# Attention scores from two-part float32r queries and keys, three products of 64 rows by 128 columns, with the image buffers placed behind attention

## The chip, the cores and the metric

The kernel runs on one core of a Trainium2 chip. A core has a matrix engine (TensorE, "PE" in the profile, with its weight loads listed apart as "PEld"), a vector engine ("DVE"), a scalar engine for activations and copies ("ACT"), a general engine ("POOL"), and a queue engine that mostly starts transfers ("SP"). Each engine works through its own list of instructions in order and waits on semaphores for the others. Data lie in SBUF (128 partitions), matrix products go to PSUM (128 partitions by 8 banks; one bank holds 512 float32 per partition), and DRAM is reached by DMA. The metric is the device time of one execution in microseconds. All runs named here agree within 0.3%.

## The reference

The input `x` is one image of 48 channels by 128 by 128 pixels in float32. Four layers are applied, each as `x = x + layer(groupnorm(x))`: an attention over pixels, four sweeps of a 5-tap convolution over rows and columns, a patch-wise convolution with normalisation, and a state-space scan. The change lies in the first layer, which is:

```python
qkv = jnp.einsum('bchw,oc->bohw', x, qkv_w)                  # 48 -> 144 channels
qkv = conv_general_dilated(qkv, dw_w, ..., 'SAME', ...)      # 3x3 depthwise
q, k, v = jnp.split(qkv, 3, axis=1)                          # 16384 tokens of 48 each
q = _l2norm(q)
k = _l2norm(k)
attn = jnp.einsum('bnc,bmc->bnm', q, k) * temperature
attn = jax.nn.softmax(attn, axis=-1)                         # 16384 x 16384
out = jnp.einsum('bnm,bmc->bnc', attn, v)
return jnp.einsum('bchw,oc->bohw', out, proj_w)
```

So every one of 16384 queries meets every one of 16384 keys: two products, each of 16384 by 16384 by 48, with an exponential between them.

## The kernel before

The program lays the four layers one after another: `attention`, `sweeps`, `patch_conv`, `scan`. Two large SBUF buffers, `xa` and `xb`, are handed from one to the next (a layer calls them `xq` and `other`).

**Inside `attention`, the convolution stage.** The image is loaded by eight DMAs into `xb`, the first half of the rows in partitions 0 to 47, the second in 64 to 111. The stage then works in eight bands of 16 rows; each band in two iterations of 1024 tokens (two chunks of `CH` = 512). `band(b)` normalises 18 rows on DVE (line 93), and copies them by DMA into shifted partitions. `conv` makes q, k and v of the 1024 tokens on PE in plain float32. `take` squares them on ACT, sums over channels on PE (the matrix `blk`), takes the root on ACT, and then DVE does, per chunk, `tensor_scalar_max` (L300), `reciprocal` (L302), and two products that write the scaled q into `xq` and k into the lower half of `xb` (L304, L307). One iteration later ACT copies q a second time, into partitions 64 to 127 of `xq` (`again`). The keys thus lie in two halves: tokens 0 to 8191 in partitions 0 to 63, the others in 64 to 127, and the queries in both.

**The attention loop, `attend`.** It runs over 32 chunks `c` of 512 queries, and inside over 64 key tiles `j`. A key tile is 128 keys of each half. `scores(c, j)` makes, in four float32 products of 49 rows by 64 columns (the four quarters of the array), a PSUM tile `s` of 128 partitions by 2 by 512; ACT makes `e = exp(absT * s)` of it; `sums(acc, j, e)` multiplies it by the values, again in four products of 64 by 64, which accumulate over `j` in the PSUM tile `acc`. PE's order is written out by `InOrder`: the scores of tile `j`, then the sums of tile `j - 2` (`BEHIND`). There are three `s` tiles (six banks), one `acc` (two banks), and five `e` buffers. At the end of a chunk ACT copies `acc` to `o`, and `divide` and `result` (DVE, with small DMAs on SP) make the chunk's output, which stays in `xq` for the sweeps and goes by DMA to `x1` in DRAM. A second loop, `attend_shifted`, stands in the other branch of `tc.If` and isn't executed with this temperature.

**After attention.** `sweeps` takes group statistics (line 71 and on), keeps PE at work meanwhile with `keep_running` (line 99), fills the borders of its buffer by POOL memsets (L678 to L683), and ACT writes the normalised image from `xq` into `xb`, 8 rows at a time. The weights `l1_w` were loaded at the program's start.

Of the kernel before, what the change touches and what calls it, by code (L numbers as in the profile page):

```python
# [20 lines left out]
F16 = mybir.dt.float16  # L21
AF = mybir.ActivationFunctionType
# [4 lines left out]
C = 48  # L27
H = W = 128
N = H * W
# [76 lines left out]
def packed_weights(nc, pool, name, w, dw, cols):  # L106

    w1 = pool.tile([128, 4, cols], F32, name="w1")
    nc.scalar.dma_start(w1.rearrange("c t o -> c (t o)"), w)
    wt = pool.tile([128, 4, cols], F32, name=name)  # L110
    nc.scalar.dma_start(wt.rearrange("c t o -> c (t o)"), dw)
    nc.vector.tensor_mul(wt, wt, w1)
    return wt
# [6 lines left out]
def attention(ctx, tc, xq, other, x1, const, ins):  # L120
# [4 lines left out]
    ident, blk, st = const["ident"], const["blk"], const["st"]  # L125
    NQ = N // CH
    HALF = N // 2

    kv = ctx.enter_context(tc.tile_pool(name="l0_kv", bufs=1))

    k = other[:, 0:HALF]

    v = other[:, HALF:N].rearrange("p (t c) -> p t c", c=64)
# [11 lines left out]

    rp = ctx.enter_context(tc.tile_pool(name="l0_r", bufs=2))
# [3 lines left out]
    with ExitStack() as a:  # L150
        act, pe = InOrder(tc, nc.scalar), InOrder(tc, nc.tensor)
        wp = a.enter_context(tc.tile_pool(name="l0_w", bufs=1))
        sp = a.enter_context(tc.tile_pool(name="l0_a", bufs=2))
        ps = a.enter_context(tc.tile_pool(name="l0_aps", bufs=4, space=PSUM))
# [4 lines left out]
        wt = packed_weights(nc, wp, "wt", ins["l0_w"], ins["l0_dw"], 192)  # L159

        values = wt[:, :, 128:192]
        turned = wp.tile([64, 4, 128], F32, name="turned")
# [9 lines left out]
        K2 = 64 + C  # L172
        for i in range(NQ // 2 - 4):
            idle = ps.tile([128, CH], F32, name="p")
            keep_running(pe, idle, ident[0:K2], other[0:K2, i * CH : (i + 1) * CH], 1)
        halves = wp.tile([K2, NQ // 2, 6], F32, name="halves")
        for i in range(NQ // 2):
            nc.vector.bn_stats(halves[:, i, :], other[0:K2, i * CH : (i + 1) * CH])
# [3 lines left out]
        R = 16  # L182
        NB = H // R
        S = W + 2
        bands = [wp.tile([128, R + 2, S], F32, name=f"band{i}") for i in range(2)]
        rests = [wp.tile([128, R // 8, 4, W], F32, name=f"rest{i}") for i in range(2)]
# [3 lines left out]
        def band(b):  # L190
# [8 lines left out]
            for p0, p1 in [(0, 10), (10, R + 2)] if b == 0 else [(0, R + 2)]:  # L199
                for half, x in enumerate((other[0:C], other[64 : 64 + C])):  # L200
                    lo = max(first + p0, half * H // 2)
                    hi = min(first + p1, (half + 1) * H // 2)
                    if lo < hi:
                        at = half * H // 2
                        normalise(
                            nc,
                            t[0:C, lo - first : hi - first, 1 : W + 1],
                            rows(x[:, (lo - at) * W : (hi - at) * W]),
                            stats,
                        )  # L210
# [59 lines left out]
        def take(t0, p, pv):  # L270
# [5 lines left out]
            vt = sp.tile([128, CH], F32, name="vt")  # L276
# [21 lines left out]
            def scale():  # L298
                for n in range(2):
# [3 lines left out]
                    q = slice(t0 + n * CH, t0 + (n + 1) * CH)  # L303
                    nc.vector.scalar_tensor_tensor(  # L304
                        xq[0:64, q], p[n][0:64], sgn[0:64], rn[0:64], ALU.mult, ALU.mult
                    )
                    nc.vector.tensor_mul(  # L307
                        k[kb : kb + 64, tk + n * CH : tk + (n + 1) * CH], p[n][64:128], rn[64:128]
                    )
                nc.gpsimd.memset(k[kb + 32 : kb + 33, tk : tk + 2 * CH], 1.0)  # L310

            def again(copy):
                for n in range(2):
                    q = slice(t0 + n * CH, t0 + (n + 1) * CH)
                    copy(xq[64:128, q], xq[0:64, q])

            if p is not late:
                scale()
            nc.vector.tensor_copy(v[:, tv, :].rearrange("t (n i) c -> t i n c", n=2), pt)
            nc.gpsimd.memset(v[:, tv, C:64], 1.0)  # L320
            return scale, again
# [3 lines left out]
        for b in range(NB):  # L325
            nxt = band(b + 1) if b + 1 < NB else None
            for y in range(0, R, 8):
# [4 lines left out]
                if last:  # L332
                    last[1](act.copy)
# [4 lines left out]

    small = nc.values_load(absT[0:1, 0:1].bitcast(mybir.dt.int32))
    bits = int(np.float32(32.0).view(np.int32))  # L340
    with tc.If(small <= bits) as near:
        attend(tc, xq, k, v, x1, absT, ident, st, ins, last)
    with near.Else():
        attend_shifted(tc, xq, k, v, x1, absT, ident, st, ins, last)
# [17 lines left out]
def attend(ctx, tc, xq, k, v, x1, absT, ident, st, ins, last):  # L362
# [6 lines left out]
    act, pe = InOrder(tc, nc.scalar), InOrder(tc, nc.tensor)  # L369
    NQ = N // CH  # L370
    KT = N // 2 // 128
    BEHIND = 2

    ep = ctx.enter_context(tc.tile_pool(name="l0_e", bufs=BEHIND + 3))
# [9 lines left out]
    def scores(c, j):  # L384
        s = ps_s.tile([128, 2, CH], F32, name="s")
        for part, half, _ in quarters:
            b = 64 * half
            pe.matmul(
                s[part, half, :],
                lhsT=k[b : b + GAP, j * 128 + part.start : j * 128 + part.stop],  # L390
                rhs=xq[b : b + GAP, c * CH : (c + 1) * CH],
                start=True,
                stop=True,
            )
# [15 lines left out]
    class Finish:  # L410
# [24 lines left out]
        def result(self):  # L435
            y = self.y[0:C]
            nc.vector.tensor_mul(y, y, self.rec)
            nc.vector.tensor_add(xq[0:C, self.cols], y, self.xres)
            nc.vector.bn_stats(st[:, self.c, :], xq[0:C, self.cols])
            if self.c < NQ - 1:  # L440
                nc.sync.dma_start(x1[:, self.cols], xq[0:C, self.cols])
# [1401 lines left out]
```

## Time and profile before

| what | us |
|---|---|
| median of three runs (7403.55 to 7419.28) | 7405.37 |
| profiled execution, its own time | 7415.31 |
| its span, first to last instruction | 7413.5 |
| start and statistics of the image | 0 to 35 |
| convolution stage | 35 to 247 |
| attention loop | 247 to 3768 |
| end of attention to the first sweep | 3768 to 3785.5 |
| sweeps and patch convolution | 3785.5 to 4700 |
| scan | 4700 to 7413.5 |

The stages were cut where the first and last products of each lie in the timeline. In the listing of instruction groups, a row gives the line, the engine and operation, the result and its inputs, the shapes, the count, then the busy time of the group in us, the mean of one in ns, and the idle time of that engine ahead of it with what ended it. Line 48 is the helper `InOrder`, through which most PE and ACT instructions are issued, so rows are told apart by their tiles. A float32 product stands in the records as two MATMULs, so the 8192 score products of the program are 16384 rows. The duration of one MATMUL contains its latency; what PE needs for one is read from the distance of starts in the timeline.

### The profile page before, as it was taken

The page shows a single profiled execution, that of the slowest core. Times are in us where ns is not written, and L with a number is a line of the kernel's source. Part 1 is how long each engine was busy: PE and PEld are TensorE (multiplying, and loading weights), DVE is VectorE, ACT ScalarE, POOL GpSimd, SP SyncE. Part 2 cuts the span into 40 slices and gives each one's busy share as a digit, 9 for nine tenths or more (in the row PEclk, how much of TensorE's full clock was granted, in tenths as well). Part 3 has the DMA queues.
Part 4 walks back from the last instruction along what each step waited for, and adds up shares of the span by engine and source line. Part 5 has one row for each costly group of instructions (what it writes and reads, how often), then busy time and mean ns, then how long its engine had stood idle before and what let it go on. Part 6 is the DMA issues. An engine that isn't in the chain of part 4 may idle for free.

```text
span 7413.5 us, 220408 instructions
## 1 busy us (share of the span) xinstructions
PE 6051.7 (82%) x101970; PEld 3057.1 (41%) x101970; DVE 3451.0 (47%) x3031; ACT 4389.3 (59%) x4744; POOL 2804.1 (38%) x603
## 2 busy tenths in 40 slices
PE   8999999999999999999999999455555545554555
PEld 3333333333333333333357855243444333343444
DVE  7300000000000000000034544699999999999998
ACT  2566666666666666666644023566666666666665
POOL 1000000000000000000010222599999999999998
PEclk9999999999999999999999999677667767766666
DMA  3000000000000000000000020465566566666775
GB/s 67 8 4 5 4 3 4 5 3 4 4 3 5 4 3 4 5 3 5 4 11 20 3 49 18 108 165 151 166 156 165 152 159 160 162 158 165 180 179 146
DMA packets 182436, 485.73 MB, mean 66 GB/s; under 512 B 35971, under 2 KB 67762, under 8 KB 179602
## 3 DMA queue, kind: packets, MB, share of 16 engines
q1 hardware_dynamic: 174679, 464.21, 24.6%
q8 instruction: 799, 13.09, 0.8%
q10 hardware_dynamic: 6827, 7.35, 0.4%
q14 instruction: 131, 1.07, 0.1%
HBM read 427.91 MB, written 22.02 MB: 61 GB/s over the span
## 4 chain that ended last, share of the span: by engine, by line
PE 61%; DVE 22%; issue 7%; POOL 5%; ACT 2%; DMA 2%; SPq 0%; ACTq 0%; DVEq 0%; POOLq 0%
PE acc L48 24%; PE s L48 24%; DVE h L1590 20%; PE p L48 7%; POOL h L1583 4%; PE y L48 3%; DMA du<-rep 1%; PE pv L48 1%; PE pp L48 1%; PE pc L48 1%; PE po L48 1%; DVE xb L48 1%; ACT dA L48 1%; ACT xb L48 1%; DVE y L48 0%
## 5 line engine op out<-in xcount | busy, mean ns | idle before, releaser
L48 ACT ACTIVATE e<-s,absT 128x1024 f32<-128x1024 f32 x2048 | 2279.5, 1115 | 1194.9 <-PE s L48 1194.0
L1583 POOL TENSOR_TENSOR h<-du,bt 128x3072 f32<-128x3072 f32 (+1 forms) x386 | 2559.9, 6676 | 94.2 <-ACT h L48 47.4
L48 PE MATMUL s<-xa,xb 49*64 49x512 f32 x16384 | 2118.1, 588 | 1.3 <-POOL xb L320 1.3
L48 PE MATMUL acc<-e,xb 64*64 64x512 f32 x16384 | 2118.1, 588 | 1.0 <-ACT e L48 1.0
L1590 DVE TENSOR_TENSOR_SCAN h<-dA,carry,h 128x1024 f32<-128x1024 f32 x864 | 1940.5, 2324 | 49.1 <-ACT dA L48 33.7
L48 ACT ACTIVATE dA<-dt,a 128x1024 f32<-128x1024 f32 x1152 | 1287.2, 1118 | 868.1 <-DVE h L1590 856.9
L48 PE MATMUL y<-h,cw 128*32 128x48 f32 x49152 | 905.9, 246 | 954.2 <-issue 513.8
L421 DVE TENSOR_TENSOR both<-o 128x512 f32<-128x512 f32 x31 | 21.5, 692 | 2963.2 <-ACT o L48 2859.5
L681 POOL MEMSET xb<- 32x2064 f32 x8 | 14.5, 1818 | 3500.4 <-PE acc L48 3491.3
L48 PEld LDWEIGHTS y<-h,cw 128*32 128x32 f32 x49152 | 815.1, 140 | 1081.6 <-issue 672.9
L48 PEld LDWEIGHTS s<-xa,xb 49*64 49x64 f32 x16384 | 616.0, 132 | 1146.1 <-issue 588.9
L48 PEld LDWEIGHTS acc<-e,xb 64*64 64x64 f32 x16384 | 615.7, 132 | 1146.8 <-issue 1123.3
L1590 DVE TENSOR_TENSOR_SCAN h<-dA,h 128x1024 f32<-128x1024 f32 x288 | 634.5, 2268 | 46.0 <-ACT dA L48 37.6
L48 PE MATMUL yz<-ev,sel 128*8 128x48 f32 x4096 | 192.1, 259 | 267.9 <-ACT ev L48 266.7
L48 PEld LDWEIGHTS yz<-ev,sel 128*8 128x8 f32 x4096 | 162.3, 106 | 326.1 <-ACT ev L48 296.4
L48 PE MATMUL p<-xb,l_w 112*48 112x78 f32 (+8 forms) x6096 | 227.5, 224 | 19.3 <-DVE xb L48 8.9
L48 PE MATMUL p<-xa,l_w 112*48 112x78 f32 (+8 forms) x6096 | 227.5, 224 | 14.4 <-DVE xa L48 5.5
L48 PEld LDWEIGHTS p<-xb,l_w 112*48 112x48 f32 x6096 | 194.5, 124 | 52.9 <-DVE xb L48 35.4
L48 PEld LDWEIGHTS p<-xa,l_w 112*48 112x48 f32 x6096 | 193.8, 123 | 48.1 <-DVE xa L48 33.7
L48 PE MATMUL pc<-wt,xa 128*128 128x288 f32 x768 | 198.0, 415 | 0.0
L783 POOL TENSOR_TENSOR xb<-xb,xa 48x2048 f32<-48x2048 f32 (+2 forms) x10 | 45.0, 4503 | 386.4 <-DVE xa L48 363.2
L48 DVE TENSOR_TENSOR xb<-p,xb 112x79 f32<-112x79 f32 (+7 forms) x508 | 114.6, 226 | 129.4 <-PE p L48 113.5
(204 smaller groups left out, 3106.3 us busy)
## 6 DMA issues: line engine op xcount, KB each, us to landing
du<-rep SPq DMA_DIRECT2D x768, 256.0 KB
dt<-rep SPq DMA_DIRECT2D x768, 256.0 KB
rep<-dd SPq DMA_DIRECT2D x24, 192.0 KB
yd<-ys ACTq DMA_DIRECT2D x256, 12.0 KB
rest<-xa SPq DMA_DIRECT2D x90, 38.0 KB
xb<-in_x_dram SPq DMA_DIRECT2D x8, 384.0 KB
xres<-in_x_dram SPq DMA_DIRECT2D x32, 96.0 KB
x<-xa SPq DMA_DIRECT2D x32, 96.0 KB
```

What stands on the lines that cost most here:

```text
L48: ins = method(*args, **kwargs).ins
L421: nc.vector.tensor_add(self.both, o[:, 0], o[:, 1])
L681: nc.gpsimd.memset(b[32:64, some, inside], 1.0)
L783: nc.gpsimd.tensor_add(xr, xr, u[0:C, x : x + xr.shape[2], E : E + H].rearrange("c w h -> c h w"),)
L1583: nc.gpsimd.tensor_mul(h[:, p, ks], du.unsqueeze(1).to_broadcast([128, ks.stop - ks.start, LC]), r["bt"][:, ks],)
L1590: nc.vector.tensor_tensor_scan(h[:, p, k, :], dA, h[:, p, k, :], carry[:, i, k : k + 1] if ci else 0.0, ALU.mult, ALU.add,)
```

## The change

Queries and keys are each split on the chip into a high part, rounded to `float32r`, and the rest, also `float32r`: `hq`, `lq`, `kh`, `kl`. A score is then made of three products in place of one: `kh` with the high query, `kl` with the high query, and both key parts with the low query. 64 rows are used in each: the channel order of q and k is turned (16 to 47, 0 to 15, and 0 to 15 once more), so that the third product and parts of the first two share rows; for the third, 32-row pieces of `kh` and `kl` are put below one another in the tiles `rest_k`. Each product now covers 64 rows by all 128 columns, and the two key halves take the upper and lower rows of the array.

The parts of the query go to a DRAM buffer `qm`, from which `moving(c)` loads a chunk by eight DMAs, one chunk ahead. Order on PE: the scores of `G` = 4 key tiles, then the sums of the four tiles before. There are seven `e` buffers. The sums are as they were. The image lies in four tiles of its own, `xa` and `xb` are laid out only after attention, the sweeps read the attention's result back from `x1` through two stage buffers, and `l1_w` is loaded after attention.

```diff
-def attention(ctx, tc, xq, other, x1, const, ins):
+def attention(ctx, tc, x1, mp, const, ins):
+    images = ctx.enter_context(tc.tile_pool(name="l0_x", bufs=1))
+    for i in range(HALF // PART):
+        t = images.tile([128, PART], F32, name=f"x{i}")
...
+    kh, kl = (kv.tile([128, HALF], F32R, name=n) for n in ("kh", "kl"))
+    def moving(c):
+        m = mp.tile([128, 2, CH], F32R, name="m")
+        high, low = qm[0:C, c * CH : (c + 1) * CH], qm[C:, c * CH : (c + 1) * CH]
+        for half in range(2):
+            at = 64 * half
+            for i, to, x in (
+                (0, 0, high),
+                (0, C, low[C:]),
+                (1, 0, low[0:32]),
+                (1, 32, low[0:32]),
+            ):
+                nc.sync.dma_start(m[at + to : at + to + x.shape[0], i].bitcast(F32), x)
+        return m
+    def join(cols):
...
+        for half in range(2):
+            at = 64 * half
+            for n, t in enumerate((kh, kl)):
+                nc.sync.dma_start(
+                    rest_k[i][at + 32 * n : at + 32 * n + 32, to].bitcast(F32),
+                    t[at : at + 32, cols].bitcast(F32),
+                )
...
+                for half in range(2):
+                    for i, x in enumerate(image):
+                        at = half * H // 2 + i * PART // W
+                        lo = max(first + p0, at)
+                        hi = min(first + p1, at + PART // W)
+                        if lo < hi:
+                            normalise(
...
-                nc.gpsimd.memset(k[kb + 32 : kb + 33, tk : tk + 2 * CH], 1.0)
-            def again(copy):
-                    copy(xq[64:128, q], xq[0:64, q])
+            def split(act, get):
+                for n in range(2):
+                    f = own[n]
+                    hq, lq = (get(name, n)[qb : qb + 64] for name in ("hq", "lq"))
+                    fq, fk = f[qb : qb + 64], f[kb : kb + 64]
+                    act.copy(hq.bitcast(F32R), fq)
+                    act.copy(kh[kb : kb + 64, at], fk)
+                    nc.gpsimd.tensor_sub(lq.bitcast(F32R), fq, hq)
+                    nc.gpsimd.tensor_sub(kl[kb : kb + 64, at], fk, kh[kb : kb + 64, at].bitcast(F32))
+                    nc.sync.dma_start(qm[0:C, to], hq[0:C])
+                    nc.sync.dma_start(qm[C : 64 + C, to], lq)
+                if kb:
+                    join(slice(tk, tk + 2 * CH))
+            def get(name, n):
+                pool = {"f": fp, "hq": once, "lq": sp}[name]
+                return pool.tile([128, CH], F32, name=name)
...
-    def scores(c, j):
+    def scores(m, j):
         s = ps_s.tile([128, 2, CH], F32, name="s")
-        for part, half, _ in quarters:
-            b = 64 * half
-            pe.matmul(
-                s[part, half, :],
-                lhsT=k[b : b + GAP, j * 128 + part.start : j * 128 + part.stop],
-                rhs=xq[b : b + GAP, c * CH : (c + 1) * CH],
+        for n in range(3):
+            k, at = key_tile(keys, n, j)
+            for half, part in enumerate(sides):
+                pe.matmul(
+                    s[:, half, :],
+                    lhsT=k[part, at],
+                    rhs=m[part, n // 2],
+                    start=(n == 0),
+                    stop=(n == 2),
...
-        for j in range(KT):
-            waiting.append((c, j, scores(c, j)))
-            while len(waiting) > BEHIND:
+        for g in range(KT // G):
+            es = [(j, scores(m, j)) for j in range(g * G, (g + 1) * G)]
+            if g == 0 and c + 1 < NQ:
+                ahead = moving(c + 1)
+            if c == 0 and g == 1:
+                split(act, get)
+            for i, e in behind:
+                if i == 0:
+                    acc = ps_a.tile([128, 2, CH], F32, name="acc")
+                sums(acc, i, e)
+            if c and g == 0:
+                finish = Finish(c - 1, acc)
...
+def key_tile(keys, n, j):
+    if n < 2:
+        return keys[n], slice(j * 128, (j + 1) * 128)
+    per = keys[2][0].shape[1] // 128
+    return keys[2][j // per], slice(j % per * 128, (j % per + 1) * 128)
...
-    keep_running(nc.tensor, idle, const["ident"], some, 6)
+    idle, some = idle[:, 0:128], const["blk"]
+    keep_running(nc.tensor, idle, const["ident"], some, 16)
...
+    for r in range(0, H, 8):
+        x = stage.tile([128, 2, CH], F32, name="m").rearrange("c a b -> c (a b)")[0:C]
+        nc.sync.dma_start(x, x1[:, r * W : (r + 8) * W])
...
-        attention(tc, xa, xb, x1, const, ins)
+    stage = ctx.enter_context(tc.tile_pool(name="stage", bufs=2))
+    attention(tc, x1, stage, const, ins)
     with ExitStack() as image:
         xp = image.enter_context(tc.tile_pool(name="image", bufs=1))
         const["l1_w"] = xp.tile([128, 3, 3, 64 + C], F32, name="l1_w")
+        nc.sync.dma_start(const["l1_w"], ins["l1_w"])
...
-    blk[:64, :64] = blk[64:, 64:] = 1.0
+    blk[:C, :64] = blk[64 : 64 + C, 64:] = 1.0
+    def turned(a):
+        return np.concatenate([a[:, 16:], a[:, :16], a[:, :16]], 1)
```

The branch that isn't executed, `attend_shifted`, is changed in the same sense. `patch_conv` and `scan` keep their work; the first rows of their hand-over, `const["x3"]`, lie in the two stage buffers in place of a buffer of their own.

## The prediction

> **What bounds the kernel now.** I read the busy time by stage first (columns: stretch in us; its length, then busy time and instruction count of PE, PEld, DVE, ACT, POOL; granted clock; DMA share; GB/s):
>
> ```profile
> core 0: us, PE busy (x) PEld busy (x) DVE busy (x) ACT busy (x) POOL busy (x), PEclk, DMA share, GB/s
> 247.00:3768.00 3521.00, 3520.10 (x32744) 1230.69 (x32744) 217.04 (x197) 2323.94 (x2113) 12.81 (x13) 1.00 0.02 4
> 35.00:247.00 212.00, 209.62 (x672) 78.18 (x672) 186.37 (x150) 66.11 (x114) 21.20 (x32) 0.97 0.24 42
> ```
>
> Attention is 3521 of 7413.5 us, and PE is busy in all of it at clock 1.00; ACT has a third of its time free and DMA is nearly idle. The groups of instructions say what PE does there and that it hardly ever waits:
>
> ```profile
> L48 ACT ACTIVATE e<-s,absT 128x1024 f32<-128x1024 f32 x2048 | 2279.5, 1115 | 1194.9 <-PE s L48 1194.0
> ...
> L48 PE MATMUL s<-xa,xb 49*64 49x512 f32 x16384 | 2118.1, 588 | 1.3 <-POOL xb L320 1.3
> L48 PE MATMUL acc<-e,xb 64*64 64x512 f32 x16384 | 2118.1, 588 | 1.0 <-ACT e L48 1.0
> ```
>
> The busy sums overlap, so the price comes from the timeline (start, duration), one key tile from it:
>
> ```profile
> 2000.78 1.04 PE L48 MATMUL s<-xa,xb 49*64 49x512 f32 x8
> 2001.21 0.15 PEld L48 LDWEIGHTS acc<-e,xb 64*64 64x64 f32 x4 [0.28 <-issue]
> 2001.64 1.04 PE L48 MATMUL acc<-e,xb 64*64 64x512 f32 x8
> ...
> 2001.97 1.11 ACT L48 ACTIVATE e<-s,absT 128x1024 f32<-128x1024 f32 x1 [0.58 <-PE s L48]
> ...
> 2002.50 1.04 PE L48 MATMUL s<-xa,xb 49*64 49x512 f32 x8
> ```
>
> Starts are 0.86 us apart: scores 0.86, sums 0.86, 1.72 for a key tile, and 2048 x 1.72 = 3523, the whole stage. Eight records run as two sets of four at once (four quarters of the array), 0.43 a set. ACT starts 0.33 after the 0.86 of its tile are over (2001.64 to 2001.97).
>
> The last view is PE in one iteration of the convolution stage, the only place where shapes alternate without waits:
>
> ```profile
> 106.34 0.60 PE L48 MATMUL pt<-ident,vt 128*128 128x128 f32 x4
> 106.78 5.32 PE L48 MATMUL p<-band,wt 128*128 128x512 f32 x12
> 112.02 1.13 PE L48 MATMUL p<-rest,wt 48*128 48x512 f32 x4
> 113.08 2.80 PE L48 MATMUL pv<-band,wt 128*64 128x512 f32 x12
> 115.81 1.08 PE L48 MATMUL pv<-rest,wt 48*64 48x512 f32 x4
> 116.81 1.98 PE L48 MATMUL pss<-sq,blk 128*128 128x512 f32 x4
> 118.64 0.60 PE L48 MATMUL pt<-ident,vt 128*128 128x128 f32 x4
> ```
>
> Full-array records take 0.43 each, so 12 should last 5.15, not 5.24. Four records of 48 rows run two at a time, upper and lower rows: 0.86, and 1.06 pass. The extra at the five changes of shape is 0.09, 0.20, 0.15, 0.14 and 0.11 us.
>
> **What the Trainium skill says.** "FP8 and Floating Point Precision", TensorE Precision Notes: true FP32 takes four passes, while a reduced form reads four bytes and truncates to FP22. The trace agrees on the four: two records a product, 0.43 each for 512 columns, are four passes of 0.215. "TensorE: Matmul & The Clock Gate", Back-to-back issue gap: N/2.4 + 2.5 ns, which for 512 columns is 0.216 us a pass. That agrees too. That a float32r product is one such pass no row here shows. "TensorEngine Tiling (Array Packing)", Key Properties: a change of tiling mode drains the engine. The 0.09 to 0.20 above fit. Same TensorE page, LDWEIGHTS: time goes with columns, and loads are pulled ahead of running products; 128-column loads of two row groups last 0.19 in the trace (the pairs staggered by 0.11), under 0.216, so they should stay hidden.
>
> **The change part by part**, per group of four key tiles; 512 groups.
>
> *Scores.* Removed: 4 x 0.86 = 3.44 us. Added: 4 tiles x 3 products, the two halves at once: 12 pairs at p. With p = 0.216, 2.59. The bounds of p: 0.213 (512 columns at 2.4 GHz, from the page), and 0.43 (a record of before that reads the same four-byte operand; a pass may not be able to go faster than that). I take 0.216, the pass that the trace implies.
>
> *A new wait.* Four score tiles run in a row, but there are three `s` buffers. The fourth can start only when ACT has emptied the first. The first tile's scores end at 3p = 0.65; ACT starts 0.30 to 0.33 later (taken: 0.30), needs 1.115, and PE restarts 0.06 after ACT ends plus some 0.10 to load weights anew (after `o` the copy ends at 3768.41, the record starts at 3768.47, and its third weight load is 0.09 late). So the fourth tile starts at 3p + 1.575 = 2.22, not at 9p = 1.94: 0.28 us a group. Bounds: 0 and 0.4. Behind the waiting product stand the fourth tile and the sums of four tiles. With it, the scores of a group last 6p + 1.575 = 2.87. Before, the sums between two tiles covered this.
>
> *Sums*: as before, 3.44. Their `e` inputs are from the group before, long done. ACT, 4 x 1.115 = 4.46 a group, stays below PE. The fourth exponential needs the `e` buffer that the first sums free, at about 3.9 to 4.2; it could start at 4.29. Free, by little; if late, it still has more than 2 us before its `s` tile is asked for.
>
> *Two changes of mode a group* (halves to quarters and back). Before: none. 0.15 each, from the rows above: 0.30. Bounds: 0 and 0.21 each.
>
> Sum of a group: 2.87 + 3.44 + 0.30 = 6.61; 512 x 6.61 = 3384 against 3523: **-139 us**.
>
> *End of a chunk.* The copy of `acc` (1.00) now stands on ACT ahead of the next group's first exponential, which it delays by about 0.36; the fourth tile passes that on: 31 x 0.36 = **+11**. Before, two score tiles covered it. The loop's start, eight score tiles ahead of any sums, waits for exponentials: **+1**.
>
> *Queries through DRAM.* Eight DMAs a chunk, 0.5 MB in some 105 us, on SP's queue behind `xres` and small `recs` and output DMAs, a chunk ahead: hidden. Without that cover, a few us a chunk.
>
> *Convolution stage.* In two iterations DVE has 2 x 11.0 (0.79 + 6.7 + 1.48 + 1.38 + 0.69 for maximum, reciprocal, the products and the copy) + 2.5 (one band) = 24.6, and PE 2 x 12.29 = 24.6: level. A band now needs up to three pieces; a one-row piece costs 0.34 in the timeline of DVE, so 2 x 0.34 x 7 = **+5**. ACT: four copies of 0.61 for two, 1.2 more on some 4.2 in 12.3: hidden. POOL: four subtractions, about 1.1 each (6.676 for 3072 elements), minus a memset of 1.12: hidden. SP gains four to eight DMAs an iteration, between those of the bands; bands have an iteration to spare. The last queries and joins land late: **+2** ahead of the first score.
>
> *After attention.* The read-back of `x1` is ready ahead of the statistics; 8 rows need 2.4 us on ACT and perhaps 3 with the load, while a sweep takes some 0.95 a row. `l1_w`, 0.5 MB, has the 19 us from 3767 to 3785. The waiting products were six of 512 columns, which the statistics' product at 3781.71 stood behind for 2 us after DVE had finished (3779.65); 16 of 128 are shorter: **-2**. Layers 2 and 3 stay.
>
> Sum: -139 + 11 + 1 + 5 + 2 - 2 = -122. The span goes from 7413.5 to 7291, the profiled time from 7415.3 to 7293. The median of the runs is 10 lower than that time: 7405 - 122 = **7283 us**.
>
> **The rivals.**
>
> *Float32r streams at half rate* (ends slower). A four-byte operand may be read at 512 columns in 0.43, and float32's two passes a record would hide in that. For it: the transposes, one record each, pass 128 columns in 0.11, the same 0.84 ns a column. Against: 128 weights are loaded for each of them too, at 0.11 a load, which explains it as well; and the precision page gives four passes, not a reading limit, as the price of FP32. Then 12 x 0.43 = 5.16 (the `s` wait vanishes), group 5.16 + 3.44 + 0.30 = 8.90, stage 4557: +1034, and 8456 us with the rest. The sign turns earlier: 512 groups must stay under 3523 - 17 = 3506, so 6p + 1.575 under 3.11, p under 0.256. A pair at 0.26 already loses, say because weights don't load side by side.
>
> *The new costs are smaller.* If float32r at 64 by 128 and float32 at 64 by 64 change without a drain and PE restarts at once: 2.77 + 3.44 = 6.21, stage 3180, near 7080; with half of both, 7180. For it: changes in the trace went down to 0.09. Against: five changes, five gaps, and the wait follows from durations that are measured.
>
> *The convolution stage becomes ACT's.* `hq` has one buffer, so ACT's second copy waits for POOL and a DMA of the first, some 2 to 3 us, ahead of the next squares on ACT's queue. PE needs those squares only after 3.8 us of v products. If they come 2 us too late, 16 x 2 = +32: 7315.
>
> **How the numbers follow.** About 0.2%, 15 us, is what a measurement of this kernel can tell from no change. Forecast, 7200 to 7375, with the convolution rival in it: 0.60. Smaller costs, 7110 to 7200: 0.16. Just faster, 7375 to 7390: 0.04. Within 0.2%: 0.04. Slower by a little (p or the changes of mode dearer than priced, to 7550): 0.06. Half rate: 0.10. Faster 0.80, same 0.04, slower 0.16. The range 7110 to 7430 holds the first four and a part of the fifth.
>
> **What would show it.** Starts of score pairs 0.216 apart; the fourth tile of a group 0.28 late, released by ACT; groups 6.6 apart; gaps of 0.15 between scores and sums; attention 3390 to 3410 long; the convolution stage 5 longer; the rest as it was. Pairs at 0.25 or more make the prediction wrong, and so do changes of mode over 0.3.

## The result, and the profile after

The changed kernel takes 7399.25 us in the median of 20 runs (7389.48 to 7410.48), against 7411.58 us for the kernel before (20 runs, 7403.29 to 7419.28). The ratio is 0.9985, with a 95% interval from 0.9979 to 0.9992: faster by 12 us, where 122 were forecast. The profiled execution took 7389.48 us, its span 7387.6, which is 26 less than that of before.

The busy time of the attention stage, cut at the first score and at the end of attention (columns as in the table before: stretch, length, busy time and instructions of PE, PEld, DVE, ACT, POOL, clock, DMA share, GB/s), and PE's two main groups in it:

```profile
core 0: us, PE busy (x) PEld busy (x) DVE busy (x) ACT busy (x) POOL busy (x), PEclk, DMA share, GB/s
246.00:3752.00 3506.00, 3473.87 (x28672) 1662.96 (x28672) 220.87 (x199) 2225.35 (x2121) 10.10 (x8) 1.00 0.03 9
```

```profile
L49 PE MATMUL acc<-e,v 64*64 64x512 f32 x16384 | 1877.4, 596 | 0.0
...
L49 PE MATMUL s<-m,kh 64*128 64x512 f32 x4096 | 943.9, 443 | 26.3 <-DMA m<-qm 15.4
```

Attention still fills PE. It lasts 3506 us where 3390 to 3410 were forecast. PE is busy in 3474 of them, so some 32 us of standing still are new; before there was almost none. Waits for `m`, 21.5 us, and two stops at the start of the loop, 9.5 us, make up 31 of them; both are shown below. A float32r product stands in the records once (4096 for 64 key tiles, 32 chunks and two halves), where a float32 product stands twice. Where the time goes within a group of four key tiles is read from PE's timeline, here one group and the first score of the next:

```profile
2004.11 0.50 PE L49 MATMUL s<-m,kh 64*128 64x512 f32 x2
...
2004.45 0.40 PE L49 MATMUL s<-m,kl 64*128 64x512 f32 x2
...
2004.68 0.39 PE L49 MATMUL s<-m,x 64*128 64x512 f32 x2
...
2006.34 0.19 PEld L49 LDWEIGHTS s<-m,kh 64*128 64x128 f32 x2 [0.33 <-ACT e L49]
...
2006.68 0.39 PE L49 MATMUL s<-m,kl 64*128 64x512 f32 x2
...
2007.24 3.66 PE L49 MATMUL acc<-e,v 64*64 64x512 f32 x32
...
2010.83 0.50 PE L49 MATMUL s<-m,kh 64*128 64x512 f32 x2
```

A pair (the products of the two halves, side by side) follows the one before after 0.23 us, but the first pair after a pause or a change of shape takes 0.34. The fourth tile starts 2.23 after the first, released by ACT. The sums and the change behind them take 3.59. The group is 6.72 us, against 4 x 1.72 = 6.88 before: 0.16 saved, not the 0.27 forecast. It stands for the others: the median over some 420 groups of the loop is 6.72 too.

A chunk is longer than its 16 groups. One copy of `acc` to `o` is made at each chunk's end (before and after; minimum, median and maximum in ns, then the first and the last start):

```profile
L48 ACT COPY o<-acc x32: 1004/1004/1012, 357.0 to 3767.4; 128x1024 f32<-128x1024 f32 x32
...
L49 ACT COPY o<-acc x32: 1012/1015/1017, 371.0 to 3751.6; 128x1024 f32<-128x1024 f32 x32
```

One period is (3751.6 - 371.0) / 31 = 109.05, and 16 x 6.72 are 107.5. SP's timeline around one end of a chunk, PE's at the same place, and the waits of SP and PE (total us, times, longest) show the rest:

```profile
1992.60 3.55 SPq L174 DMA_DIRECT2D m<-qm  x8
```

```profile
1992.49 3.66 PE L49 MATMUL acc<-e,v 64*64 64x512 f32 x32
...
1996.09 0.50 PE L49 MATMUL s<-m,kh 64*128 64x512 f32 x1
...
1996.91 0.46 PE L49 MATMUL s<-m,kh 64*128 64x512 f32 x1 [0.33 <-DMA m<-qm]
...
1997.89 0.46 PE L49 MATMUL s<-m,x 64*128 64x512 f32 x1 [0.26 <-DMA m<-qm]
```

```profile
SPq L174 <- PE s L49: 2441.1, 30, 81.8
...
PE s L49 <- DMA m<-qm: 21.5, 55, 1.9
```

SP waits up to 82 us for PE's scores, 30 times in all, and starts the eight loads of the next chunk's queries at 1992.60, when the last scores of the running chunk have just ended (the sums that follow them start at 1992.49). PE wants those queries 3.5 us later; two loads haven't landed, and it stops twice. The first group of the chunk takes 8.0 us, from 1996.09 to 2004.11 (the first line of the group above), instead of 6.72.

At the start of the loop PE stands still twice, for 4.5 and 5.0 us:

```profile
253.10 0.79 PE L49 MATMUL s<-m,kh 64*128 64x512 f32 x2 [4.54 <-ACT e L49]
...
253.70 0.63 PE L49 MATMUL s<-m,kl 64*128 64x512 f32 x2
...
254.13 0.63 PE L49 MATMUL s<-m,x 64*128 64x512 f32 x2
...
268.60 3.13 ACT L49 ACTIVATE e<-s,absT 128x1024 f32<-128x1024 f32 x3 [4.01 <-POOL kl L378]
...
269.76 0.80 PE L49 MATMUL s<-m,kh 64*128 64x512 f32 x2 [4.99 <-ACT e L49]
...
271.34 5.29 PE L49 MATMUL acc<-e,v 64*64 64x512 f32 x32
```

It waits for ACT both times. ACT makes its first exponential only at 251.9, behind late rounded copies. Later it waits 4.0 us itself, until POOL has made the last part of the keys (`kl`) from the last iteration's q and k; by the program these lie in three of the seven `e` buffers. After each stop PE comes back at about half its pace: pairs are 0.43 apart, and 32 sums take 5.29 us instead of 3.66.

The last place is the start of the sweeps. The timeline of ACT, POOL and PE there, and under it one of POOL's border memsets in the profile of before:

```profile
3764.10 0.20 ACT L421 ACTIVATE absT<-absT 128x1 f32<-128x1 f32 x1
...
3764.41 0.76 POOL L787 MEMSET xb<- 128x256 f32 x2 [3495.85 <-PE idle L100]
...
3781.38 0.32 POOL L792 MEMSET xb<- 48x128 f32 x1
...
3781.76 15.76 PE L49 MATMUL p<-xb,l_w 112*48 112x50 f32 x368 [12.00 <-POOL xb L792]
```

```profile
3752.90 1.82 POOL L681 MEMSET xb<- 32x2064 f32 x1 [7.52 <-PE s L48]
```

PE begins the sweeps at 3769.05 and stands still from the next step until POOL has set the last border of the whole buffer, 12.0 us. Before, POOL was at these borders at 3752.90 already, while attention ran until 3767.4.

The books over the two profiled executions, each row with the forecast's value for it:

| stretch | before | after | change | forecast |
|---|---|---|---|---|
| first convolution product to first score | 201.0 | 206.5 | +5.5 | +7 |
| first score to first copy of `acc` | 113.6 | 124.8 | +11.2 | -3 |
| 31 periods: groups (31 x 16 x -0.16) | | | -79 | -135 |
| 31 periods: what a chunk adds to its groups | -2 | 47 | +49 | +11 |
| last copy of `acc` to first sweep product | 18.1 | 17.5 | -0.6 | -2 |
| first half of the sweeps | 245.3 | 254.8 | +9.5 | 0 |

The forecast's 5 and 2 us of the convolution stage and its end stand together in the first row. The rows sum to -4; with the first convolution product 2.7 earlier in this execution that is the -6.9 seen where the second half of the sweeps starts. From the start of the scan to the end the profile of before shows 2672 us and this one 2652. The code there is the same but for where its first input rows lie, and the ten profiles of changed kernels in this study lie between 2652 and 2668 there. Part of these 20 us is chance: the profiled execution of before took 4 us more than the median of its runs, and this one 10 less. The 26 us between the profiles are therefore no measure; the 12 of the runs are. The books place 4 of these 12. The other 8 aren't placed. The stretch from the second half of the sweeps to the scan differs by only 1 us, and the first convolution product starts between 39.7 and 43.3 in the changed kernels, around the 42.4 of before. The scan could hold them, since the one profile of before is longer there than all ten others, but no run shows that it does.

### The profile page after: what moved, and what is told of

Same layout as the page of the kernel before. It is cut to its first block, busy times and chain, and to the rows that moved or that the text cites. A ratio compares the mean times of both kernels' runs of the same rounds, so it can differ in the third digit from the quotient of the medians.

```text
span 7387.6 us, 213035 instructions
## 1 busy us (share of the span) xinstructions
PE 5986.4 (81%) x97900; PEld 3479.6 (47%) x97900; DVE 3451.2 (47%) x3043; ACT 4305.3 (58%) x4776; POOL 2867.1 (39%) x651
## 4 chain that ended last, share of the span: by engine, by line
PE 58%; DVE 24%; issue 6%; POOL 5%; DMA 3%; ACT 2%; SPq 2%; ACTq 0%; DVEq 0%; POOLq 0%
PE acc L49 23%; PE s L49 22%; DVE h L1704 21%; PE p L49 7%; POOL h L1697 4%; PE y L49 2%; SPq L174 1%; DMA du<-rep 1%; DMA m<-qm 1%; DVE xb L49 1%; PE pc L49 1%; PE po L49 1%; ACT dA L49 1%; PE pv L49 1%; DVE y L49 0%
## 5 line engine op out<-in xcount | busy, mean ns | idle before, releaser
L49 ACT ACTIVATE e<-s,absT 128x1024 f32<-128x1024 f32 x2048 | 2171.0, 1113 | 1229.5 <-PE s L49 1131.8
L49 PE MATMUL acc<-e,v 64*64 64x512 f32 x16384 | 1877.4, 596 | 0.0
L498 DVE TENSOR_TENSOR both<-o 128x512 f32<-128x512 f32 x31 | 21.5, 692 | 2948.3 <-ACT o L49 2948.3
L49 PEld LDWEIGHTS acc<-e,v 64*64 64x64 f32 x16384 | 576.8, 133 | 1037.2 <-issue 1036.8
L49 PE MATMUL s<-m,kh 64*128 64x512 f32 x4096 | 943.9, 443 | 26.3 <-DMA m<-qm 15.4
L49 PE MATMUL s<-m,x 64*128 64x512 f32 x4096 | 831.8, 390 | 6.4 <-DMA m<-qm 6.0
L49 PE MATMUL s<-m,kl 64*128 64x512 f32 x4096 | 830.2, 392 | 0.0
L49 PEld LDWEIGHTS s<-m,kh 64*128 64x128 f32 x4096 | 398.1, 184 | 660.8 <-issue 392.3
L49 PEld LDWEIGHTS s<-m,x 64*128 64x128 f32 x4096 | 403.1, 185 | 102.9 <-DMA m<-qm 18.1
L49 PEld LDWEIGHTS s<-m,kl 64*128 64x128 f32 x4096 | 401.3, 186 | 42.1
```

Of the source, the lines that this page charges most:

```text
L49: ins = method(*args, **kwargs).ins
L498: nc.vector.tensor_add(self.both, o[:, 0], o[:, 1])
```

## The experiments

The theory after the result: the pairs and the sums are near what was forecast, and the gain is eaten by four things at different places: (1) late loads of `m`, (2) POOL's borders behind attention, (3) a slow start of the loop, (4) a group that is 0.11 dearer, put down to the changes of shape. What each run was expected to show, and its rival, stand ahead of its result.

**A buffer of its own for the first chunk's queries.** The stage pool has two buffers, but the first chunk's `m` is taken ahead of `tc.If` and is read in both branches.

```diff
-    def moving(c):
-        m = mp.tile([128, 2, CH], F32R, name="m")
+    def moving(c, pool=mp):
+        m = pool.tile([128, 2, CH], F32R, name="m")
...
-    first = moving(0)
+    first = moving(0, kv)
```

> The changed kernel, but the first chunk's queries m get a buffer of their own, so that the two buffers of the stage pool are both free for the chunks after it. Theory (the first buffer is held for the other branch, so one buffer turns and each chunk's eight loads start only when the last scores of the chunk before are done): the loads go out in a chunk's first group, the period of a chunk falls from 109.05 to about 107.6 us (16 groups of 6.72 and 0.1 for the copy of the sums), the waits of PE for m vanish, and the time falls by 31 x 1.45 = 45 us. Rival (the chunk's end is long because ACT copies acc ahead of the next exponentials, 1.0 us): the period stays at 108.5 or more and the time falls by 15 us at most.

Measured: 7351.62 us (ratio to before 0.9925, 0.9911 to 0.9938), 48 less than the changed kernel. The period of a chunk is (3705.7 - 371.6) / 31 = 107.55, no wait of PE for `m` is left, and SP's timeline shows the loads at the other end of a chunk:

```profile
1976.10 4.20 SPq L174 DMA_DIRECT2D m<-qm  x8
```

They start when the scores of a chunk end, as before, but the chunk that follows begins at 1979.6 with queries that are there already: these loads are for the one after it. So the theory holds: the first chunk's tile keeps a buffer from the later chunks. That it does so because both branches read it was not tried apart. The rival falls: ACT's copy of `acc` costs a chunk nothing measurable (107.55 against 16 x 6.72 = 107.52).

**The last border block by block.**

```diff
             nc.gpsimd.memset(b[0:C, some, E - 1 : E], 0.0)
-        nc.gpsimd.memset(b[64:K, lines, E + W - 1 : E + W], 0.0)
+            nc.gpsimd.memset(b[64:K, some, E + W - 1 : E + W], 0.0)
```

> The changed kernel, but the last memset of the borders (the two columns at the rows' ends, 48 partitions) is made in each block of 16 rows, right behind that block's others, instead of once behind all blocks. Theory (the image's buffer lies in the memory of the attention, so POOL's memsets come after its end and the sweeps stand still until the last of them): the sweeps' wait of 12.0 us for POOL goes, their second step starts at about 3769.5 instead of 3781.8, and all that follows is 12 us earlier. Rival (the reading back of x1 by rows would stop the sweeps just as long): less than 4 us are gained, and PE's wait is then put down to ACT or to the load of m.

Measured: 7386.86 us (0.9970, 0.9959 to 0.9981), 12 less than the changed kernel, as the theory said, though the two intervals touch. The trace is clearer. In this execution all stands 7 us later. The sweeps begin at 3776.49 and go on:

```profile
3776.49 0.89 PE L49 MATMUL p<-xb,l_w 112*48 112x78 f32 x24 [2.08 <-POOL xb L791]
...
3777.61 7.42 PE L49 MATMUL p<-xb,l_w 112*48 112x76 f32 x168 [0.22 <-DVE xb L49]
```

The first half of the sweeps lasts 242.4 instead of 254.8. The read-back of `x1` doesn't take the place of the wait. Why POOL starts only at 3764.4 is told less surely: the profile of the changed kernel puts its wait down to the waiting products (`idle`), and that of this run to a third instruction, but the waits of the run with the first chunk's buffer name `absT`'s square root on ACT. This fits best: in all three profiles the first memset starts 0.11 us after that square root ends (3764.30 and 3764.41 above):

```profile
POOL xb L787 <- ACT absT L421: 3449.4, 1, 3449.4
```

**The start of the loop.** POOL instead of ACT makes the rounded copies of the last two iterations.

```diff
-                    act.copy(hq.bitcast(F32R), fq)
-                    act.copy(kh[kb : kb + 64, at], fk)
+                    cast(hq.bitcast(F32R), fq)
+                    cast(kh[kb : kb + 64, at], fk)
...
-                    last[1](act, last[2])
+                    final = (b, y) == (NB - 1, R - 8)
+                    last[1](nc.gpsimd.tensor_copy if final else act.copy, last[2])
...
-                split(act, get)
+                split(nc.gpsimd.tensor_copy, get)
```

> The changed kernel, but POOL instead of ACT makes the rounded copies (hq, kh) of the last two iterations of the convolution stage. Theory (ACT's late copies and hq's single buffer hold the first exponential back to 251.9, PE stands still for 4.5 us and comes back at half clock): ACT begins the first exponential at about 247.5, PE doesn't pause, pairs of scores stay 0.23 apart instead of 0.43, and the first sums start at about 249.5 instead of 258.8: 9 us less in all. Rival (the first chunk then waits for the late queries and keys, which POOL makes 4 x 0.6 us later): the gain is given back within the first chunk, and the copy of its sums ends where it did, 2 us either way.

Measured: 7395.26 us (0.9981, 0.9974 to 0.9988), no different from the changed kernel (0.9979 to 0.9992). PE's timeline:

```profile
258.99 0.76 PE L49 MATMUL s<-m,x 64*128 64x512 f32 x1 [5.82 <-DMA m<-qm]
```

Neither theory nor rival had this wait in it. The loads of the first chunk's `m` stand on SP's queue behind the transfers of the iteration that POOL now finishes later, and PE waits 5.8 us for one of them. The first wait for ACT was replaced by one for SP; the second was shorter here, 1.9 us.

**Groups of two.**

```diff
-    G = 4
+    G = 2
```

> The changed kernel with groups of two key tiles instead of four. Three score buffers then suffice, so no score waits for an exponential, and the changes between 64 rows by 128 columns and 64 by 64 are doubled. Theory (each group pays 0.36 us for its two changes: 0.21 from scores to sums and back into the first pair's loading, 0.15 behind the sums; and 0.17 for the fourth tile): a group of two takes 6 x 0.23 + 1.72 + 0.36 = 3.46 us against 3.36 for half a group of four, 1024 x 0.10 = 100 us slower than the changed kernel, 7500. Rival (the gaps of 0.15 and 0.11 come of the wait for the fourth tile, not of the change of shape): 3.10 to 3.2 us, 150 us and more faster than the changed kernel.

Measured: 7586.02 us (1.0242, 1.0228 to 1.0256), 187 more than the changed kernel. The group, from first score to first score:

```profile
2000.25 0.50 PE L49 MATMUL s<-m,kh 64*128 64x512 f32 x2
...
2001.84 1.95 PE L49 MATMUL acc<-e,v 64*64 64x512 f32 x16
...
2003.72 0.50 PE L49 MATMUL s<-m,kh 64*128 64x512 f32 x2
```

It takes 3.47, as the theory said. The gaps stay with no score waiting for an exponential, so that wait is not what they come of: 0.11 in the first pair, 0.10 ahead of the sums, 0.15 behind them. But 1024 x (3.47 - 3.36), some 110 us, are not 187. The period of a chunk is (3940.8 - 377.1) / 31 = 114.96, 4.0 more than 32 groups. So the time was only half explained.

**Groups of two with the first chunk's buffer.** Both edits together, to see whose the other 80 us were.

> Groups of two, and the first chunk's queries in a buffer of their own. Groups of two alone were 187 us slower than the changed kernel, of which 1024 groups of 3.47 explain 108; the period of a chunk was 114.96, 4.0 more than 32 groups of 3.47. Theory (the rest is the late loads of m, which cost more here because only two score tiles of the next chunk can't be cut short: PE stands still and comes back at half clock): with the loads in time the period is 111.0 to 111.2, and the time about 7400 - 45 + 105 = 7460. Rival (groups of two pay at a chunk's end for ACT's copy of acc, which stands ahead of the two exponentials that the next sums wait for): the period stays over 112.5, the time over 7500.

Measured: 7450.83 us (1.0052, 1.0035 to 1.0068). The copies of `acc`:

```profile
L49 ACT COPY o<-acc x32: 1012/1014/1017, 373.6 to 3804.1; 128x1024 f32<-128x1024 f32 x32
```

The period is (3804.1 - 373.6) / 31 = 110.66, as long as 32 groups: the late loads had cost groups of two 114.96 - 110.66 = 4.3 us a chunk. So the late loads are dearer in groups of two, and a comparison of group sizes with them in would have given a wrong price. In the run before this one PE stops longer for them and comes back at half pace, here with a granted clock of 0.51 from 1983 to 1990 us:

```profile
1983.36 0.79 PE L49 MATMUL s<-m,kh 64*128 64x512 f32 x1 [2.68 <-DMA m<-qm]
```

Its waits of PE for `m` sum to 66.8 us, against 21.5 in groups of four.

**Two products a score.** The product of `kl` with the high query is left out.

```diff
-        for n in range(3):
+        for n in (0, 2):
```

> The changed kernel with two products a score tile instead of three: the product of the keys' second part (kl) with the queries' first part is left out of the computation. Theory (the fourth tile of a group starts when ACT has emptied the first score buffer, not when the products before it are done): a group goes from 6.72 to about 6.2 to 6.3 us, since the fourth tile then starts at 2.0 instead of 2.26 and ends 0.23 sooner after that; 512 x 0.47 = 240 us less. Rival (the 12 pairs set the pace): four pairs of 0.23 fewer, 0.92 a group, 470 us less.

Measured: 7180.61 us (0.9691, 0.9676 to 0.9706), 219 less than the changed kernel. The group:

```profile
2006.35 0.50 PE L49 MATMUL s<-m,kh 64*128 64x512 f32 x2
...
2008.38 0.50 PE L49 MATMUL s<-m,kh 64*128 64x512 f32 x2 [0.38 <-ACT e L49]
...
2012.64 0.50 PE L49 MATMUL s<-m,kh 64*128 64x512 f32 x2
```

Four pairs fewer should give 0.92 a group if the pairs set the pace. The group falls by 0.43, from 6.72 to 6.29: the fourth tile starts at 2.03 instead of 2.23, when ACT has read the first buffer, with PE standing still for 0.38 before it. The wait that the prediction put there is real.

**The same bytes as bfloat16.** Shapes, order and waits unchanged; only the upper two bytes of each operand are used.

```diff
-                    lhsT=k[part, at],
-                    rhs=m[part, n // 2],
+                    lhsT=k.bitcast(BF16)[part, 2 * at.start + 1 : 2 * at.stop : 2],
+                    rhs=m.bitcast(BF16)[part, n // 2, 1::2],
```

> The changed kernel with the same bytes read as bfloat16: each operand of the score products is the upper half of the four-byte value, every second element of its row, so the low bits of both parts are left out. Shapes, order, buffers and waits stay. Theory (the 0.23 between pairs is that of two row groups by turns with 128 columns of weights each, whatever the type): pairs stay 0.23 apart, the group stays at 6.7, the time within 15 us of the changed kernel's. Rival (0.014 of it is float32r's own, in reading or in loading weights): pairs 0.216 apart or less, 6 x 0.014 and some of the 0.11 of a first pair saved, 6.5 to 6.65 a group, 35 to 110 us less.

Measured: 7288.56 us in a single run, 111 less than the changed kernel, whose 20 runs spread over 21 us. The group:

```profile
2006.32 0.40 PE L50 MATMUL s<-m,kh 64*128 64x512 bf16 x2
...
2006.56 0.39 PE L50 MATMUL s<-m,kl 64*128 64x512 bf16 x2
...
2006.79 0.39 PE L50 MATMUL s<-m,x 64*128 64x512 bf16 x2
...
2008.14 0.09 PEld L50 LDWEIGHTS <-kh 64*128 64x128 bf16 x1
...
2008.44 0.40 PE L50 MATMUL s<-m,kh 64*128 64x512 bf16 x2
...
2012.82 0.40 PE L50 MATMUL s<-m,kh 64*128 64x512 bf16 x2
```

The rival won, though not as it was put: pairs are 0.225 apart, hardly less than 0.23. What falls is the first pair, 0.24 instead of 0.34. The weights of one half of the fourth tile are loaded at 2008.14, 0.30 ahead of the product that uses them, while PE waits for ACT; in the changed kernel both halves' loads start with their products, at 2006.34. But the gain doesn't need that: at the group's first score (2006.32 and 2012.82) both bfloat16 loads start with their products too, and the pair is 0.24 all the same. What differs at both places is the load's own time, 0.09 us for 128 columns of bfloat16 and 0.18 for float32r. The group is 6.50, and 512 x 0.22 = 113 us are about the whole difference. So some 0.2 of a group belong to float32r at the two places where PE starts anew. That its weights cost this, and not its queries, is read from the durations; the run changes the type of both.

**All three repairs**, with the first chunk's loads issued ahead of the last transfers.

```diff
                     final = (b, y) == (NB - 1, R - 8)
+                    if final:
+                        first = moving(0, kv)
```

> The changed kernel with three repairs together: a buffer of its own for the first chunk's queries, the last memset of the borders block by block, and the rounded copies of the last two iterations of the convolution stage made by POOL, here with the loads of the first chunk's queries issued ahead of those iterations' transfers on SP's queue (in the run where POOL made the copies, the loads stood behind them, and PE waited 5.8 us). Theory (the three costs lie one behind the other in time, so the gains add): 45 + 12 + 9 = 66 us less than the changed kernel, 7333. Rival (the start is bound by the last keys and queries anyway): the start gives nothing, 7342 or more.

Measured: 7346.98 us (0.9918, 0.9904 to 0.9931), 52 less than the changed kernel and only 5 less than the first chunk's buffer alone, a difference smaller than the spread of either run (7341.69 to 7351.50 and 7347.14 to 7354.11). The first half of the sweeps fell from 251.5 to 242.1 beside that run. The start, from first convolution product to first copy of `acc`, fell from 331.3 in the changed kernel to 327.6, 4 us and not 9: ACT's first exponential comes 3.4 earlier in the stage, and the eight tiles that stand ahead of any sums then wait for ACT's exponentials one by one. PE's first stop shrinks from 4.5 to 1.2 us, but the second, which the theory had left out, stays: 5.3 us, again for an exponential that waits for POOL, and again with a clock of 0.5 behind it. The period of a chunk is 107.67, 0.12 longer than with the buffer alone, which takes the 4 us away again; why was not tried.

**The sums in float32r too.** All three repairs; `e` and `v` are rounded to float32r once, their low parts are left out; both halves go to one bank. `acc` then takes one bank instead of two and gets a second buffer, and ACT copies less at a chunk's end.

```diff
-        for part, half, to in quarters:
+        for half in range(2):
             pe.matmul(
-                acc[to, part.start // 64, :],
-                lhsT=v[part, half * KT + j, :],
-                rhs=e[part, half, :],
-                start=(j == 0),
-                stop=(j == KT - 1),
+                acc,
+                lhsT=v[:, half * KT + j, :],
+                rhs=e[:, half, :],
+                start=(j == 0 and half == 0),
+                stop=(j == KT - 1 and half == 1),
             )
```

> All three repairs, and the sums over keys as float32r too: exponentials and values are rounded to float32r once (their low parts are left out), one product of 128 rows by 64 columns for each half of the keys and key tile, both into one bank. Theory (a float32r product of 512 columns takes 0.216 to 0.23 whatever its rows): sums of a group take 8 x 0.23 = 1.84 instead of 3.44, the group 3.13 + 1.84 + 0.15 = 5.1 us, 512 x 1.6 = 820 us less than with the repairs alone, about 6510. Rival A (with full rows a four-byte operand streams at half rate, 0.43): 8 x 0.43 = 3.44, no gain but the copies' few us, about 7330. Rival B (ACT becomes the bound and adds its copy of the sums): between, 5.3 us a group and more.

Measured: 6523.12 us (0.8801, 0.8788 to 0.8814), 824 less than with the repairs alone. Stage and group:

```profile
251.00:2890.00 2639.00, 2630.69 (x16384) 1589.53 (x16384) 179.67 (x137) 2135.49 (x2081) 9.15 (x10) 1.00 0.04 11
```

```profile
2005.53 0.50 PE L49 MATMUL s<-m,kh 64*128 64x512 f32 x2
...
2008.66 2.06 PE L49 MATMUL acc<-e,v 128*64 128x512 f32 x8
...
2010.65 0.50 PE L49 MATMUL s<-m,kh 64*128 64x512 f32 x2
```

The eight products and the change behind them take 1.99 us instead of 3.59, the group 5.12 instead of 6.72. Full rows stream no slower than half rows. PE stays the bound; ACT has 500 of 2639 us left. This is the fastest kernel of the study, 886 us below the kernel before in its own comparison, but it computes with fewer bits than the change under study, which kept the low parts.

## Why the prediction was wrong

The forecast of 7283 was 116 us below the result. Its range, 7110 to 7430, holds the result, but to what came, a change within 0.2%, it gave a chance of 0.04, and its own signs of being wrong (pairs at 0.25 or more, changes of mode over 0.3) did not show. Two steps failed and carry most of the miss: float32r weight loads "should stay hidden" (in *A new wait*), and the next chunk's queries are "hidden" (in *Queries through DRAM*). Two that were put at next to nothing, the loop's start and the end of attention, carry the rest. Step by step:

*Scores.* Right in kind: one pass a product, halves side by side. The pitch is 0.23 where 0.216 was taken. The rival of half rate, 0.43 a pair, is dead. The pitch stayed under 0.256, where the sign of the whole change was said to turn: the groups alone gain 512 x 0.16 = 82 us.

*A new wait.* The place and the releaser were right: the fourth tile was put at 2.22 and starts at 2.23, and leaving out a product moves it to 2.03. That the number fits so closely is luck. The first tile takes 0.80 where 0.65 was put, and the 0.10 for loading weights anew does not stand ahead of the restart, as the sum had it, but in the restarted pair; the two errors cancel. The second one comes due behind the restart: that pair takes 0.34, so the fourth tile needs 0.90 to the start of the sums, where 3 x 0.216 and a change of 0.15 made 0.80. The step leaned on the Trainium skill, "TensorE: Matmul & The Clock Gate", Part 2: What happens when you issue a matmul, by which PE pulls weight loads ahead of running products; the prediction took from it that they stay hidden. Between running pairs the trace agrees: the load for the pair of 2006.91 starts at 2006.69, during the pair before, and the pitch is 0.23. At a restart float32r's load starts with its product, as at 2006.34, and isn't hidden. The measurement decides. The prediction priced such a load once a group, at 0.10; it is there twice, at 0.11 each.

*Sums* and *Two changes of mode a group* held: 3.59 for the sums and the change behind them, as forecast; 0.10 for the other change instead of 0.15. The group as a whole is 6.72 instead of 6.61, 57 us over 512 groups. This is the largest part of the miss.

*End of a chunk*, +11 for ACT's copy of `acc`: mis-sized, it costs nothing. ACT in a group with the copy, and at the first exponential of the next group:

```profile
2004.25 1.01 ACT L49 COPY o<-acc 128x1024 f32<-128x1024 f32 x1 [1.40 <-PE acc L49]
...
2005.17 3.13 ACT L49 ACTIVATE e<-s,absT 128x1024 f32<-128x1024 f32 x3
...
2011.90 3.12 ACT L49 ACTIVATE e<-s,absT 128x1024 f32<-128x1024 f32 x3 [1.69 <-PE s L49]
```

The first exponential starts 1.06 after the group's first score with the copy (2004.11 to 2005.17) and 1.07 without (2010.83 to 2011.90).

*Queries through DRAM.* This step failed in its mechanism. "A chunk ahead: hidden" was read from the order of the program, in which the call does stand a chunk ahead. When the load can start is set by when its buffer comes free, and the first chunk's tile, shared by both branches, kept one of two buffers. The step itself named the price, "a few us a chunk" without its cover; it was 1.5 a chunk, 47 us, and the run with a separate buffer took 48 back. That the first chunk's tile holds the buffer is what that edit shows; that PE's scores release the loads stands in SP's waits above.

*The loop's start*, +1: it is +14 (the first chunk's 11.2, and the 2.6 that its 16 groups gain). The step saw that eight score tiles wait for exponentials, but not what holds ACT back: ahead of the first, its own late copies and the single buffer of `hq`, which the rival on the convolution stage had named for another place; and later the last iteration's keys on POOL. PE stops twice and comes back at half clock each time; the granted clock is 0.50 from 253.0 to 257.5 and from 269.8 to 274.6. "TensorE: Matmul & The Clock Gate", Part 1: The HAM clock gate, says that an idle window of about 3.4 us halves the clock, and the trace agrees. The edit that shrank the first stop gave back 4 us; what the second costs is read from the timeline alone, since no edit removed it by itself.

*Convolution stage*, +5 and +2 ahead of the first score: +5.5 in all, near enough; what it is made of was not tried. The rival that it becomes ACT's, at +32, fell.

*After attention*, -2: it is +9. The step weighed the read-back of `x1`, the load of `l1_w` and the waiting products, but not POOL's borders, which the new place of the image moves from under attention to behind it: eight blocks of 16 rows and their pads, 17 us in all, of which the sweeps saw 12. Setting one border in another order took all 12 back.

Between the forecast's -122 and the -4 of the books lie 118 us: the groups are 56, the chunk ends 38 (49 for the late loads, less the 11 for a copy that costs nothing), the start 14, and the sweeps with what lies ahead of them 11; together 119, less 1.5 by which the convolution stage was cheaper. The chunk ends and the sweeps were confirmed by edits of their own, the groups by the timeline and the bfloat16 run; of the start an edit confirmed 4.

## What to carry to other kernels

A load that the program issues early starts when its buffer is released, so count the buffers that really turn, and leave out one that a tile from ahead of the loop still holds. When memory is handed to another stage, list every instruction that used to run under the old stage because its memory was free: here a row of memsets. And when a phase is made of short stretches, price the first instruction of each stretch apart from the steady pitch; two such starts cost 0.2 us in a group of 6.7, more than the 0.16 that the group gained.

## What the runs showed of the hardware that was not expected

- A pair of float32r products of 512 columns, 64 rows by 128 columns each, takes 0.23 us. Of 128 rows by 64 columns, eight single products and the change behind them take 1.99 us, about as much for each. As bfloat16 the pairs are 0.225 apart, so four bytes an element cost 2% of the rate here.
- At a restart, the first float32r pair takes 0.11 us longer than the next ones, a bfloat16 pair 0.01 to 0.02. A load of 128 columns lasts 0.18 us as float32r and 0.09 as bfloat16.
- A change between 64 by 128 and 64 by 64 cost 0.10 in one direction and 0.15 in the other, in every group looked at and for both group sizes.
- PE pauses of 4.5, 5.0 and 5.8 us were followed by pairs 0.43 apart.
